# Half-array products issued in turn, an earlier load of pole planes, and two banks at the end of layer 1

## The chip, the core and the metric

The kernel runs on one core of a Trainium2 chip. The metric is the device time of one execution in microseconds (us). Engines are named PE (TensorE: matrix products; PEld are its weight loads), DVE (VectorE), ACT (ScalarE), POOL (GpSimd) and SP (SyncE, which here only issues transfers). L313 is line 313 of the kernel before.

## The reference

The input x is 16 images x 16 channels x 256 x 256, in 32-bit floats. Two layers each add a function of the group-normed x (8 groups of two channels) to x. Cut to what matters here:

```python
# layer 0, v = _gn(x)
alpha = fft2(v)
A = 1 / (omega1[:, None, None, None] - weights_pole1[None])
Bm = 1 / (omega2[:, None, None, None] - weights_pole2[None])
S = einsum('ikpq,oikp,xikq->oxik', weights_residue, A, Bm)
output_residue1 = einsum('biox,oxik->bkox', alpha, S)
C = einsum('biox,oikp->bikpx', alpha, A)
D = einsum('bikpx,xikq->bikpq', C, Bm)
output_residue2 = einsum('bikpq,ikpq->bkpq', D, weights_residue)
x = x + ifft2(output_residue1).real + pole_part(output_residue2) / Nx / Ny
# layer 1, v = _gn(x)
f = mish(conv2d(v, W1, b1))             # 3x3, each channel alone, 4 features
top, bot = upper and lower half of f
ti = involution of top with a kernel made from bot
out = mish(conv2d(concat(ti, roll(bot, -1)), W2, b2))
gate = sigmoid(3 taps over the channels of out.mean(axis=(2, 3)))
x = x + v * gate
```

The Fourier transforms are done as products with tables of cosines and sines; the spectrum is kept for 33 groups of four row frequencies.

## The kernel before

Four functions run one after the other; each takes its on-chip memory afresh, so that its first loads wait until those who last used that memory are done.

**layer0_forward** goes through 64 steps (16 images, four channels at a time). In a step, `rows` transforms the rows of the four channels (products pu and pv, lines 207 and 214) and ACT makes v from pv; `poles` multiplies v with a table into pd (line 241); and `columns` transforms the columns of the image before, two or three calls a step, into px (line 313), which ACT copies to o (line 320) and GpSimd stores to al in DRAM (line 329). The order of TensorE's instructions is written out by hand (`manual_schedule`); the other engines' orders are laid by a scheduler. The outputs pd and px have two halves of 64 partitions: a product with 64 weight columns fills the left or the right half of the array, and its output lies in partitions 0 to 63 or 64 to 127. Before, all products of one half are issued, and then all of the other: in `poles` the loop over a (the half) lies outside that over n (four products that add up), in `columns` the loop over k (the half) outside h and part. From image 1 on the steps also carry pieces of `tables`, VectorE work that makes tables for the later stages.

**layer0_mix** loads ident, ix, m8, four pieces of tt, and then the spectrum alc (eight transfers, which read al) and the pole planes av, all on SP's queue, in that order. From av VectorE makes lt (line 621); TensorE multiplies tt and lt into ps (line 635, the two halves in turn); ACT and VectorE copy ps to s (lines 643 and 645); then they spread alc into alb (lines 592 and 594); and then the products of s and alb begin (line 657). The orders of PE, ACT, DVE and POOL are by hand here.

**layer0_back** makes the new x and its norm and is not touched.

**layer1** works on nine units per image; the second convolution of an image runs while the next image's units do. After the last image only its second convolution is left: eight calls of `conv2`, each with two groups of products (line 1111, 48 records in four quarters of the array) into one bank, c2ps, whose pool `ps2` has a single buffer. ACT applies mish and adds up (line 1120). SP loads the rows that a call reads (line 1097, two buffers). Then `gate` forms the gate, and for eight parts of the image o is loaded (line 1135, four buffers), scaled four channels at a time on GpSimd (line 1158) and stored (line 1167).

Of the kernel before, what the change touches and what calls it, by code (L numbers as in the profile page):

```python
# [19 lines left out]
N = 256  # L20
G = 8
P = 128
# [50 lines left out]
def layer0_forward(ctx, tc, d, al, bd, tabs):  # L73
# [160 lines left out]
    def poles(cg, vts, acc):  # L234

        pd = psd.tile([P, 2, P], F32, tag="pd", name="pd")
        for j, vt in enumerate(vts):
            for a in range(2):
                ch = 4 * cg + 2 * j + a
                for n, (xh, k) in enumerate(((0, 0), (0, 1), (1, 0), (1, 1))):  # L240
                    nc.tensor.matmul(
                        pd[64 * a : 64 * a + 64, j],
                        lhsT=vt[:, a, xh, 64 * k : 64 * k + 64],
                        rhs=bt[:, xh, ch, 1 - k : 3 - k].rearrange("p l m -> p (l m)"),
                        start=n == 0,
                        stop=n == 3,
                    )
        gs = slice(2 * cg, 2 * cg + 2)

        def times(out, part, coef):  # L250
            shape = [P, 2, part.shape[2] // M, M]
            nc.vector.tensor_tensor(
                out.rearrange("p g (k q) -> p g k q", q=M),
                part.rearrange("p g (k q) -> p g k q", q=M),
                coef[:, gs].unsqueeze(2).to_broadcast(shape),
                ALU.mult,
            )

        t = dp.tile([P, 2, P], F32, tag="t", name="t")
# [42 lines left out]
    def columns(b, g0, rsc):  # L302

        u = us[b % 2]
        n = min(4, NF - g0)
        o = op.tile([P, 2, 2, N], F32, tag="o", name="o")
        for j in range(0, n, 2):
            lanes = 64 * min(2, n - j)
            ps = psx.tile([P, 2, 2, H], F32, tag="px", name="px")
            for k in range(min(2, n - j)):  # L310
                for h in range(2):
                    for part in range(2):
                        nc.tensor.matmul(  # L313
                            ps[64 * k : 64 * k + 64, :, h],
                            lhsT=u[:, h, part, g0 + j + k].rearrange("p f c -> p (f c)"),
                            rhs=wxn[:, h, part],
                            start=part == 0,
                            stop=part == 1,
                        )
# [228 lines left out]
def layer0_mix(ctx, tc, d, al, hd, tabs):  # L548
# [3 lines left out]
    nc = tc.nc  # L552
    nb = d["x"].shape[0]
    cp = ctx.enter_context(tc.tile_pool(name="mc", bufs=1))
    ident = load(nc, cp, d["ident"], [P, P], "ident")
    ix = load(nc, cp, d["ix"], [P, 8, N], "ix")
    m8 = load(nc, cp, d["m8"], [P, 8], "m8")

    tt = cp.tile([P, 2, C, N], F32, name="tt")
    for k in range(0, C, 4):  # L560
        nc.sync.dma_start(out=tt[:, :, k : k + 4], in_=tabs[0][:, :, k : k + 4])
    avd = tabs[1]

    alb = cp.tile([P, N, 4, nb], F32, name="alb")
    m4 = load(nc, cp, d["m4"], [P, 4], "m4")

    ap = ctx.enter_context(tc.tile_pool(name="ma", bufs=2))
    lp = ctx.enter_context(tc.tile_pool(name="ml", bufs=1))  # L570
    gp = ctx.enter_context(tc.tile_pool(name="mg", bufs=1))
    hp = ctx.enter_context(tc.tile_pool(name="mh", bufs=3))
# [31 lines left out]
    def spread(spectrum, f):  # L604
        for eng, parts in zip((nc.scalar, nc.vector), spreads[f]):
            for q, j in parts:
                expand(spectrum[q], q, j, eng)

    def load_poles(g):
        av = ap.tile([P, 32, 4, 3], F32, tag="av", name="av")  # L610
        nc.sync.dma_start(out=av.rearrange("p k f l -> p (k f l)"), in_=avd[g])
        return av

    def poles(av):

# [101 lines left out]
    E = mybir.EngineType  # L717
    with tc.manual_schedule(engines={E.PE, E.Activation, E.DVE, E.Pool}):
        spectrum = [load_spectrum(0, q) for q in range(4)]
        lt = poles(load_poles(0))  # L720
        av = load_poles(1)
        s = gp.tile([P, N, 2, C], F32, tag="s", name="s")
        for k0 in range(0, C, 2):
# [149 lines left out]
def layer1(ctx, tc, d, zn, cf, mr, nb):  # L873
# [225 lines left out]
    def conv2(b, s, acc):  # L1099
# [3 lines left out]

        begin = ((H + 1, 1, H + 2), (0, H + 1, 1))
        for q in range(2):
            ps = ps2.tile([P, 4, H], F32, tag="c2", name="c2ps")
            for blk in range(2):
                for dx in range(3):
                    x = begin[q][dx]
# [13 lines left out]
    def gate(b, acc):  # L1123
# [29 lines left out]
        for k in range(0, 8, 2):  # L1153
            following = [part(k + 2), part(k + 3)] if k < 6 else None
            c = k // 2 * 4
            for half, o in enumerate(parts):
                for i in range(4):
                    nc.gpsimd.tensor_scalar(
                        o[:, i],
                        o[:, i],  # L1160
                        scale[:, c + i : c + i + 1],
# [274 lines left out]
```

## Time and profile before

The time is 7599.57 us, the median of three runs (7587.35 to 7604.02). The profile is of an execution of 7581.6 us.

| stretch of the profile (us) | what runs |
|---|---|
| 0 to 1415 | layer0_forward |
| 1415 to 1480 | mix's loads, first tables s and alb |
| 1480 to about 2970 | layer0_mix, 33 groups |
| about 2970 to 3820 | layer0_back |
| about 3820 to 7443 | layer1, units and second convolution |
| 7443 to 7549 | second convolution of the last image, gate |
| 7549 to 7581.6 | output pass of the last image |

| line, engine | what | count | mean ns of one |
|---|---|---|---|
| L313 PE | px, 64 weight columns, 256 moving | 4224 | 385 |
| L241 PE | pd, 64 weight columns, 128 moving | 2048 | 279 |
| L635 PE | ps, 64 weight columns, 256 moving | 4224 | 384 |
| L1111 PE | c2ps, 32 weight columns, 512 moving | 12288 | 599 |
| L1120 ACT | mish of c2ps | 256 | 687 |

The mean of one is its latency: products are pipelined and those on different parts of the array overlap, so what a product costs is read from how far apart the starts lie. A view by lines gives the busy time of such a group and what ended the idle time before it; a view by stretches shows which engine is full in a stage; the timeline shows instructions in order of time, neighbours of one kind merged.

### The profile page before, as it was taken

The numbers are of one execution on the slowest core, as the hardware profiler recorded it, in microseconds if no ns is written. First come the engines' busy times: TensorE is split into PE (matmuls) and PEld (weight loads), VectorE is DVE, ScalarE is ACT, GpSimd is POOL, SyncE is SP. The second block draws the span as 40 slices with busy tenths as digits, with TensorE's granted clock in tenths as the row PEclk, the third lists the DMA queues.
The fourth block names the chain that finished last, engine by engine and source line by source line (L and its number), as shares of the span: only waits on it lengthen the run. The fifth ranks groups of instructions, "written<-read, shape, count | busy, mean of one in ns | idle before, by whom it ended". The sixth has DMA issues, their size and how long they took to land.

```text
span 7581.6 us, 148237 instructions
## 1 busy us (share of the span) xinstructions
PE 7060.1 (93%) x58664; PEld 4076.6 (54%) x58664; DVE 4908.4 (65%) x9169; ACT 3712.2 (49%) x5659; POOL 3029.4 (40%) x4126
## 2 busy tenths in 40 slices
PE   7889999799999998999979999999999999999997
PEld 5778888566667666777733333333333333333332
DVE  8999875366666665666656666666666666666662
ACT  2223333366666664111146666666666665666662
POOL 2334444211111111111135555656555666555664
PEclk9999999899999999999989999999999999999999
DMA  3444444333333335767657788888888888888886
GB/s 97 113 115 119 119 118 111 108 97 100 100 95 96 97 97 162 251 243 250 241 151 215 228 255 254 251 265 264 244 252 256 248 267 256 249 254 254 247 266 212
DMA packets 702807, 1443.62 MB, mean 190 GB/s; under 512 B 93866, under 2 KB 520038, under 8 KB 652166
## 3 DMA queue, kind: packets, MB, share of 16 engines
q1 hardware_dynamic: 557990, 959.89, 42.3%
q0 software_dynamic: 144128, 474.25, 20.4%
q8 instruction: 468, 7.67, 0.4%
q14 instruction: 221, 1.81, 0.1%
HBM read 877.25 MB, written 556.47 MB: 189 GB/s over the span
## 4 chain that ended last, share of the span: by engine, by line
PE 67%; DVE 4%; issue 3%; ACT 3%; DMA 3%; POOL 1%; SPq 0%; DVEq 0%; POOLq 0%; ACTq 0%
PE c2ps L1111 16%; PE c L969 12%; PE pd L1037 12%; PE py L837 6%; PE ph L692 5%; PE ps L635 5%; PE pg L657 4%; PE py L840 3%; ACT wide L1017 3%; DVE alb L594 2%; PE pr L996 2%; PE pf L828 1%; DMA rows<-cf 1%; PE pt L673 1%; DMA z<-zn 1%
## 5 line engine op out<-in xcount | busy, mean ns | idle before, releaser
L1017 ACT ACTIVATE wide<-c,b 32x512 f32<-32x512 f32 x2176 | 1477.4, 679 | 353.9 <-PE c L969 302.7
L1045 DVE TENSOR_TENSOR t<-pd,r 64x512 f32<-64x512 f32 x1088 | 744.2, 684 | 1286.0 <-PE pd L1037 1263.2
L1048 DVE TENSOR_TENSOR top<-pd,t 32x512 f32<-32x512 f32 x2176 | 1503.1, 691 | 52.6
L1111 PE MATMUL c2ps<-rows,c 128*32 128x512 f32 x12288 | 1391.3, 599 | 17.8 <-ACT e L1120 15.6
L969 PE MATMUL c<-z,w 102*128 102x512 f32 x2048 | 1014.7, 628 | 135.9 <-ACT wide L1017 113.8
L1029 POOL COPY wide<-wide 32x1031 f32<-32x1031 f32 (+1 forms) x576 | 568.9, 988 | 1233.5 <-ACT wide L1017 1206.2
L1037 PE MATMUL pd<-wide,dw 128*128 128x512 f32 x2048 | 1014.4, 617 | 6.5 <-DVE top L1048 2.8
L1111 PEld LDWEIGHTS c2ps<-rows,c 128*32 128x32 f32 x12288 | 392.8, 109 | 982.3 <-issue 873.9
L969 PEld LDWEIGHTS c<-z,w 102*128 102x128 f32 x2048 | 401.1, 198 | 674.3 <-issue 485.3
L1037 PEld LDWEIGHTS pd<-wide,dw 128*128 128x128 f32 x2048 | 377.1, 194 | 614.6 <-issue 446.7
L709 POOL DMA_DIRECT2D hd<-h x254 | 188.6, 743 | 1269.3 <-DVE h L705 1249.4
L1030 POOL COPY wide<-wide 32x1031 f32<-32x1031 f32 (+1 forms) x576 | 572.2, 993 | 35.6
L1120 ACT ACTIVATE e<-c2ps,b 128x512 f32<-128x512 f32 x256 | 175.9, 687 | 834.6 <-PE c2ps L1111 831.9
L313 PE MATMUL px<-wxn,u 128*64 128x256 f32 x4224 | 558.9, 385 | 2.1 <-ACT o L320 1.8
L837 PE MATMUL py<-h,iy 128*128 128x256 f32 x2048 | 541.8, 383 | 5.2 <-DMA h<-hd 5.2
L635 PE MATMUL ps<-tt,lt 128*64 128x256 f32 x4224 | 496.5, 384 | 38.9 <-DVE lt L621 34.5
L692 PE MATMUL ph<-ix,yt 64*128 64x256 f32 x4128 | 501.6, 390 | 7.1 <-issue 6.4
L313 PEld LDWEIGHTS px<-wxn,u 128*64 128x64 f32 x4224 | 401.1, 136 | 127.5 <-ACT o L320 5.4
L837 PEld LDWEIGHTS py<-h,iy 128*128 128x128 f32 x2048 | 385.2, 191 | 108.4 <-issue 44.0
L692 PEld LDWEIGHTS ph<-ix,yt 64*128 64x128 f32 x4128 | 392.2, 189 | 93.3 <-issue 46.1
L207 PE MATMUL pu<-fy,eo 128*128 128x128 f32 x2048 | 426.0, 291 | 13.0 <-DVE u L224 8.9
L988 ACT ACTIVATE bot<-c,b 128x512 f32<-128x512 f32 x544 | 343.9, 683 | 175.2 <-PE c L969 167.3
(199 smaller groups left out, 10307.1 us busy)
## 6 DMA issues: line engine op xcount, KB each, us to landing
rows<-cf SPq DMA_DIRECT2D x128, 2176.0 KB
z<-zn SPq DMA_DIRECT2D x768, 257.8 KB
cf<-top POOLq DMA_DIRECT2D x512, 240.0 KB, 7.0
cf<-bot POOLq DMA_DIRECT2D x96, 840.0 KB, 11.5
alc<-al SPq DMA_DIRECT2D x264, 256.0 KB
zn<-zb SPq DMA_DIRECT2D x128, 516.0 KB
o<-zn SPq DMA_DIRECT2D x128, 516.0 KB
z<-in_x SPq DMA_DIRECT2D x64, 1024.0 KB
```

The source lines that it names most:

```text
L313: nc.tensor.matmul(ps[64 * k : 64 * k + 64, :, h], lhsT=u[:, h, part, g0 + j + k].rearrange("p f c -> p (f c)"), rhs=wxn[:, h, part], star ...
L635: nc.tensor.matmul(ps[64 * h : 64 * h + 64, v], lhsT=lt[:, h, k, 1 - v : 3 - v].rearrange("p l f c -> p (l f c)"), rhs=tt[:, h, k], start= ...
L692: nc.tensor.matmul(ph[q][:, e], lhsT=yt[lanes, i].rearrange("p t k -> p (t k)"), rhs=ix[lanes, i], start=n == 0, stop=n == 3,)
L837: nc.tensor.matmul(py[:, yh], lhsT=iy[:, v, ys], rhs=h[:, k, v], start=v == 0, stop=False)
L969: nc.tensor.matmul(ps[:, a], lhsT=w, rhs=z[:k, c : c + 2, 0:N], start=True, stop=True)
L1017: nc.scalar.activation(self.feat[64 - 32 * q : 96 - 32 * q, f, self.groups[g], :H], ps[q][32 * f : 32 * f + 32], AF.Mish, bias=b1[0][32 * ...
L1029: nc.gpsimd.tensor_copy(flat[0:32, f, 1:m], flat[64:96, f, 0 : m - 1])
L1030: nc.gpsimd.tensor_copy(flat[96:128, f, 0 : m - 1], flat[32:64, f, 1:m])
L1037: nc.tensor.matmul(ps, lhsT=dwt if self.tail else dw, rhs=self.feat[:, f, cs, :H], start=True, stop=True,)
L1045: nc.vector.tensor_tensor(t[64:128], ps[:64], self.r[:, cs], ALU.mult)
L1048: nc.vector.tensor_tensor(self.top[32 * f : 32 * f + 32, cs, q], ps[lanes], t[lanes], ALU.add)
L1111: nc.tensor.matmul(ps[32 * j : 32 * j + 32], lhsT=c2[:, blk, dx, :], rhs=t[:, 4 * j + blk : 4 * j + blk + 4, x : x + H], start=(blk, dx) = ...
```

## The change

Four edits. In `poles` and `columns` the loop over the half becomes the innermost, so that the products go left, right, left, right; each half keeps its own order. In mix, m8 and the first av are loaded ahead of tt, and ident and ix behind it. In the last image's `conv2` the second group of each call takes a buffer of `psd` (three buffers, otherwise used for pd) in place of the single one of `ps2`. And in the last image's output pass three of the four channels of a part are scaled by VectorE, one by GpSimd. Everything that is computed stays the same.

```diff
@@ poles
-            for a in range(2):
-                ch = 4 * cg + 2 * j + a
-                for n, (xh, k) in enumerate(((0, 0), (0, 1), (1, 0), (1, 1))):
+            for n, (xh, k) in enumerate(((0, 0), (0, 1), (1, 0), (1, 1))):
+                for a in range(2):
+                    ch = 4 * cg + 2 * j + a
                     nc.tensor.matmul(
                         pd[64 * a : 64 * a + 64, j],
@@ columns
-            for k in range(min(2, n - j)):
-                for h in range(2):
-                    for part in range(2):
+            for h in range(2):
+                for part in range(2):
+                    for k in range(min(2, n - j)):
                         nc.tensor.matmul(
                             ps[64 * k : 64 * k + 64, :, h],
@@ layer0_mix
-    ident = load(nc, cp, d["ident"], [P, P], "ident")
-    ix = load(nc, cp, d["ix"], [P, 8, N], "ix")
     m8 = load(nc, cp, d["m8"], [P, 8], "m8")
+    ap = ctx.enter_context(tc.tile_pool(name="ma", bufs=2))
+    avd = tabs[1]
...
+    av = load_poles(0)
     tt = cp.tile([P, 2, C, N], F32, name="tt")
     for k in range(0, C, 4):
         nc.sync.dma_start(out=tt[:, :, k : k + 4], in_=tabs[0][:, :, k : k + 4])
-    avd = tabs[1]
+    ident = load(nc, cp, d["ident"], [P, P], "ident")
+    ix = load(nc, cp, d["ix"], [P, 8, N], "ix")
...
-        lt = poles(load_poles(0))
+        lt = poles(av)
@@ conv2
-            ps = ps2.tile([P, 4, H], F32, tag="c2", name="c2ps")
+            pool, tag = (psd, "d") if q and b == nb - 1 else (ps2, "c2")
+            ps = pool.tile([P, 4, H], F32, tag=tag, name="c2ps")
@@ gate
-                    nc.gpsimd.tensor_scalar(
+                    eng = nc.vector if i and b == nb - 1 else nc.gpsimd
+                    eng.tensor_scalar(
```

More of the change, by code (lines that the diff above doesn't have):

```diff
@@ L554, in layer0_mix, with load_poles @@
     cp = ctx.enter_context(tc.tile_pool(name="mc", bufs=1))
-    ident = load(nc, cp, d["ident"], [P, P], "ident")
-    ix = load(nc, cp, d["ix"], [P, 8, N], "ix")
     m8 = load(nc, cp, d["m8"], [P, 8], "m8")
+    ap = ctx.enter_context(tc.tile_pool(name="ma", bufs=2))
+    avd = tabs[1]
+    def load_poles(g):
+        av = ap.tile([P, 32, 4, 3], F32, tag="av", name="av")
+        nc.sync.dma_start(out=av.rearrange("p k f l -> p (k f l)"), in_=avd[g])
+        return av
+    av = load_poles(0)
     tt = cp.tile([P, 2, C, N], F32, name="tt")
@@ L561, in layer0_mix @@
         nc.sync.dma_start(out=tt[:, :, k : k + 4], in_=tabs[0][:, :, k : k + 4])
-    avd = tabs[1]
+    ident = load(nc, cp, d["ident"], [P, P], "ident")
+    ix = load(nc, cp, d["ix"], [P, 8, N], "ix")
     alb = cp.tile([P, N, 4, nb], F32, name="alb")
     m4 = load(nc, cp, d["m4"], [P, 4], "m4")
-    ap = ctx.enter_context(tc.tile_pool(name="ma", bufs=2))
     lp = ctx.enter_context(tc.tile_pool(name="ml", bufs=1))
@@ L607, in spread @@
                 expand(spectrum[q], q, j, eng)
[L609 to L612, printed above, removed]
     def poles(av):
```

## The prediction, made before the result was known

> **What bounds the kernel now.** I began with the chain of work that ended last, to see which engine sets the end:
>
> ```profile
> PE 67%; DVE 4%; issue 3%; ACT 3%; DMA 3%; POOL 1%; SPq 0%; DVEq 0%; POOLq 0%; ACTq 0%
> ```
>
> TensorE carries two thirds of it, but the four edits sit in different stages. So next the busy time of each engine in the stretches they touch (columns: stretch, its length, then PE, PEld, DVE, ACT, POOL busy with counts, TensorE clock, DMA share, GB/s):
>
> ```profile
> 552.58:1020.87 468.29, 456.45 (x4065) 392.08 (x4064) 423.88 (x1085) 178.33 (x311) 220.99 (x300) 1.00 0.44 119
> 1020.87:1370.34 349.47, 349.47 (x3194) 304.34 (x3193) 187.30 (x568) 107.31 (x213) 166.15 (x234) 1.00 0.40 107
> 147.92:552.58 404.66, 356.58 (x2825) 311.72 (x2824) 371.62 (x1104) 110.35 (x205) 146.05 (x200) 0.92 0.41 114
> 1415.50:1480.30 64.80, 17.43 (x133) 10.32 (x136) 23.70 (x25) 19.67 (x15) 4.39 (x8) 0.65 0.44 156
> 7442.80:7548.70 105.90, 87.34 (x771) 24.52 (x770) 4.79 (x14) 15.23 (x35) 31.96 (x56) 1.00 0.64 211
> 7548.70:7581.60 32.90, 0.00 (x0) 0.00 (x0) 0.00 (x0) 0.00 (x0) 23.82 (x40) 0.50 0.57 192
> ```
>
> In the forward stage, 1020.87 to 1370.34 is pure TensorE (349.47 of 349.47; 19 steps of four channels), 147.92 to 552.58 is VectorE's (92%, 16 steps), and 552.58 to 1020.87 lies between (PE 97%, DVE 91%, 24 steps). The start of mix has TensorE working 17 of 65 us. In the tail it works 87 of 106; in the output pass GpSimd works alone.
>
> One forward step's half-array part, on TensorE's timeline (start, length, line, tiles, count):
>
> ```profile
> 1057.02 2.24 PE L241 MATMUL pd<-bt,v 128*64 128x128 f32 x29
> 1058.99 0.43 PE L313 MATMUL px<-wxn,u 128*64 128x256 f32 x1
> 1059.10 0.38 PE L241 MATMUL pd<-bt,v 128*64 128x128 f32 x2
> ...
> 1059.47 7.90 PE L313 MATMUL px<-wxn,u 128*64 128x256 f32 x62
> 1067.30 0.38 PE L34 MATMUL gn_mean<-mv,ones 128*128 128x2 f32 x2
> ```
>
> A written product is two records (two passes). The 32 pd and 64 px passes take 1057.02 to 1067.30, 10.28 us. The halves do overlap already: the first px pass, on the left half, starts before pd's last ones on the right. Read one by one, the starts go in fours: px starts come in twins, 6 ns apart, at 1003.42, 1004.34 and 1005.26, each half making four passes 0.216 apart with one interval of 0.267 where the halves change over, so eight passes take 0.920, where pairs of 0.216 would take 0.862. And since one half runs four passes behind the other, the burst's first four and last four run alone.
>
> Mix's residues already alternate the halves:
>
> ```profile
> 1821.85 1.95 PE L635 MATMUL ps<-tt,lt 128*64 128x256 f32 x16
> 1823.72 3.73 PE L692 MATMUL ph<-ix,yt 64*128 64x256 f32 x32
> ```
>
> Sixteen passes of px's shape from 1821.85 to 1823.72, 1.87 us with the turnaround; record by record pairs start every 0.216 with no interval missed but the first, 0.267.
>
> **What the Trainium skill says.** "TensorE: Matmul & The Clock Gate", Part 3, says that weight loads overlap running matmuls only when the row group differs, and that matmuls start in strict order. Here it does not hold: px at 1058.99 precedes pd at 1059.10, and ps pairs with different *column* halves run at 0.216. "TensorEngine Tiling (Array Packing)", Key Properties, says that tiles load weights and multiply independently; that agrees. "DMA: Bandwidth & Descriptors", Queues, rings and completion order, says each DMA engine consumes descriptors in ring order; it agrees with av, issued at 1436.81 behind 7 MB and used at 1447.38. "SBUF — State Buffer", two separate sides, says VectorE in a two-port mode and GpSimd exclude each other on a shared port pair; no run here shows it yet.
>
> **Forward products.** Alternating: pd 16 pairs x 0.109 (its passes' interval) = 1.74; px 32 pairs x 0.216 = 6.91; turnaround after the last pair, 0.09 over an interval (1067.30 less the last px start, 1066.99, is 0.31); two first intervals, 0.05 each; and a wait for v of the second half, ready at 0.89 (ACT 1057.21 for 0.69) plus a semaphore, when the first eight pairs are through at 0.92: 0.05. Sum 8.9, against 10.28: 1.4 us a step. No instruction is added on any engine.
> - 19 pure TensorE steps and the last: 20 x 1.4 = 28. VectorE has 187 of 349 there, so nothing takes over.
> - 24 mixed steps: 24 x 1.4 = 34 if all counted, but 468 - 34 = 434 would ask VectorE for 424 of 434. In the VectorE-bound stretch it reached 92%; at 92 to 95% the floor is 446 to 461. Gain 7 to 22; I take 14.
> - 16 VectorE-bound steps: TensorE waits there already; 0 to 6, taken 2.
> - the last image's columns after 1385: pairs save 2, but o's two buffers wait for their stores (ACT waited 7.8 on al<-o at 1422.97): 1.
>
> Forward 45, between 28 and 60.
>
> **Mix's start.** VectorE's first work and the sync queue before:
>
> ```profile
> 1447.38 3.70 DVE L621 TENSOR_TENSOR lt<-av,m 128x512 f32<-128x512 f32 x6 [64.92 <-DMA av<-avd]
> 1468.31 11.74 DVE L594 TENSOR_SCALAR alb<-alc,m 128x1024 f32<-128x1024 f32 x10
> 1479.86 2.48 DVE L621 TENSOR_TENSOR lt<-av,m 128x512 f32<-128x512 f32 x4
> ...
> 1429.79 6.94 SPq L582 DMA_DIRECT2D alc<-al  x8
> 1436.81 14.62 SPq L611 DMA_DIRECT2D av<-avd  x3
> ```
>
> Now: av lands 1447.4, residues and their copies to 1468.3, the spread to 1480.05, first mix product 1480.25. After: m8 and av (0.2 MB) are issued first at 1415.6 and land by about 1419; lt is done by 1423; the first piece of tt lands by 1422. But the first copy into s waits, in the program as built, for the semaphores of the last al stores (its memory overlaps what these read), which arrived at 1429.7; alc's issue waits for the same. So four k (psg's buffers) are computed early, and the other twelve follow from 1429.8: two to three at half clock, 1.7 each, the rest 0.86: 13 us, to 1443. The spread's quarters of alc stream in order behind the same bytes as before, so the last still lands by 1447, ahead of its use; 11.7 us more give 1454.6. Gain 25. If s did not wait, the bound is the landing of alc: 28; if every late k runs at half clock: 20. Moving ident and ix behind tt costs nothing: they are first needed at 1495, and 420 GB/s bring them by 1435.
>
> **Tail of layer 1.** The 16 product groups of the last image and the store loop:
>
> ```profile
> 7508.07 5.41 PE L1111 MATMUL c2ps<-rows,c 128*32 128x512 f32 x48 [0.96 <-ACT e L1120]
> 7514.43 5.42 PE L1111 MATMUL c2ps<-rows,c 128*32 128x512 f32 x48 [0.95 <-ACT e L1120]
> ...
> 7548.70 2.19 POOL L1158 TENSOR_SCALAR o<-o,scale,mean 128x258 f32<-128x258 f32 x4 [59.48 <-DVE scale L1151]
> 7551.19 0.79 POOL L1167 DMA_DIRECT2D out_dram<-o  x1 [0.30 <-POOL o L1158]
> 7552.02 2.19 POOL L1158 TENSOR_SCALAR o<-o,scale,mean 128x258 f32<-128x258 f32 x4
> ```
>
> Each group waits for the activation of the one before, the bank being single: 6.38 apart. With a second bank, 12 rounds of four quarters, whose starts lie 0.431 apart, are 5.2: 1.2 x 16 = 19 at most. The loads of rows then set the pace: a load (2176 KB) takes 8.4 alone but about 11 while the image before is being stored (7458 to 7500, DMA 96% busy), and one issue at 7456.7 stands behind o loads on the in-order sync queue. Followed step by step, rows of s=2 land at 7467.5 (start then, 7469.72 now: 2 gained), s=5 lands about 7503.7 (now 7508.07: 4 gained), and only the last three steps run free, 2.1 each: 10.5. Between 8 and 17.
>
> Output pass: a part now costs GpSimd 2.19 + 0.30 + 0.79 = 3.3 us. After, one row group on GpSimd (0.55), three on VectorE (about 0.35 each, from L515's 128x256), the wait and the issue: 1.7 to 2.3. Then the four reloads decide, each behind the store that frees its buffer (3.4 from issue to landing), 3.5 to 4 to arrive: last store issued at +17, landed at +21 to 22, for 32 now. Bytes agree: 6.3 MB at 400 GB/s are 16. Gain 10; 7 if the port pair serialises VectorE and GpSimd, 13 if the 2.7 us before the last store goes too. The new bank and the VectorE rows add waits, but behind them nothing else is queued.
>
> Sum: 45 + 25 + 10.5 + 10 = 91: 7600 - 91 = 7509, say 7508.
>
> **Rivals.**
> - *VectorE takes what TensorE gives.* For it: 91% busy over the mixed steps. Against: 19 steps at 54%. With only a fifth of the forward's gain: 9 + 45.5, 7545.
> - *Everything counts*, the mixed steps in full and rows never late: 28 + 34 + 6 + 28 + 17 + 13 = 126, 7474. Against: the VectorE sums above.
> - *Slower.* If two halves' weights cannot load together, each 64-column load (0.137) would follow the other: pairs of 0.274, 48 x 0.274 = 13.2 a step, 2.9 more, over 44 steps 128; less 45.5: 7682. Against: ps does it at 0.216.
>
> **How the numbers follow.** Forecast 0.75, first rival 0.14, second 0.06, slower 0.03; 0.02 for gains so far eaten that nothing is measured. The time is the forecast's. Adding the ends of the forward term (17 either way) and those of the others in quadrature gives some 20 about 7508; up to 7542 it takes in half of the first rival, down to 7484 the nearer part of the second.
>
> **What will show it.** px starting every 0.216 in pairs; the pure steps 16.7 us instead of 18.07, the mixed ones bound by VectorE at about 95%; first pg product 25 us closer to the last px; groups of c2ps 5.2 apart except where rows<-cf is named; last store 21 us after scale. The forecast fails if the pure steps keep their length (the halves were not the limit), or if ACT's drain of px becomes the wait.

## The result and the profile after

The changed kernel takes 7524.26 us, the median of five runs (7514.01 to 7531.52); the kernel before took 7599.57. The ratio is 0.9903, with a 95% interval of 0.9886 to 0.992: about 75 us less (61 to 87), where 91 were forecast. The direction and the places are as forecast, and the time lies in the range, but three of the four terms came out smaller.

The profiled execution of the changed kernel lasts 7527.5 us. Line numbers move a little: px stays L313; lt is L623 and ps L637; in layer 1 c2ps is L1115, e L1124, rows L1099, the loads of o L1139, the scaling L1163, the store L1172. First the stretches that answer to those of the prediction (stretch, length, then PE, PEld, DVE, ACT, POOL busy with counts, TensorE clock, DMA share, GB/s):

```profile
148.20:552.50 404.30, 339.18 (x2825) 285.26 (x2824) 371.03 (x1104) 110.18 (x205) 145.70 (x200) 0.91 0.41 114
552.50:1015.50 463.00, 429.64 (x4066) 354.01 (x4064) 418.65 (x1085) 177.44 (x310) 220.71 (x300) 0.98 0.45 121
1015.50:1341.40 325.90, 325.90 (x3194) 270.59 (x3192) 187.32 (x568) 107.30 (x213) 166.13 (x234) 1.00 0.43 114
1382.90:1422.10 39.20, 17.05 (x131) 11.28 (x128) 23.63 (x25) 19.68 (x15) 4.40 (x8) 0.74 0.73 248
7398.50:7498.30 99.80, 88.38 (x771) 31.67 (x770) 4.88 (x14) 15.23 (x35) 31.96 (x56) 0.94 0.67 224
7498.30:7527.50 29.20, 0.00 (x0) 0.00 (x0) 9.46 (x25) 0.00 (x0) 11.47 (x16) 0.50 0.62 216
```

A step is counted here from its first pd product to that of the next. Line by line against before: the VectorE-bound steps keep their length (404.3 for 404.7), the mixed ones lose 5 us (463.0 for 468.3), the pure ones 24 (325.9 for 349.5). The start of mix, from the last px to the first product of mix, is 39 for 65, the tail of layer 1 is 100 for 106, the output pass 29 for 33. In the mixed steps TensorE's busy time fell by 27 us (456.5 to 429.6), but the steps shortened by 5: TensorE now waits for 33 us where it waited for 12. That is where the largest missing piece of the gain went. (The tail's line also has a lower TensorE clock, 0.94 for 1.00; this comes back below.)

Half-array part of one pure step, TensorE's timeline after (start, length, line, tiles, count):

```profile
1048.92 2.04 PE L241 MATMUL pd<-bt,v 128*64 128x128 f32 x32
1050.79 7.08 PE L313 MATMUL px<-wxn,u 128*64 128x256 f32 x64
1057.79 0.38 PE L34 MATMUL gn_mean<-mv,ones 128*128 128x2 f32 x2
```

From 1048.92 to 1057.79 are 8.87 us; before it took 10.28, and 8.9 were forecast.

The last image's second convolution and the output pass after, on TensorE's and GpSimd's timelines (in brackets the idle time before, and what ended it):

```profile
7398.60 21.12 PE L1115 MATMUL c2ps<-rows,c 128*32 128x512 f32 x192
7424.76 33.71 PE L1115 MATMUL c2ps<-rows,c 128*32 128x512 f32 x288 [5.03 <-DMA rows<-cf]
7462.13 33.05 PE L1115 MATMUL c2ps<-rows,c 128*32 128x512 f32 x288 [3.66 <-DMA rows<-cf]
```

```profile
7498.48 0.55 POOL L1163 TENSOR_SCALAR o<-o,scale,mean 128x258 f32<-128x258 f32 x1 [53.78 <-DVE scale L1155]
7500.56 0.79 POOL L1172 DMA_DIRECT2D out_dram<-o  x1 [1.53 <-issue]
...
7508.39 0.67 POOL L1163 TENSOR_SCALAR o<-o,scale,mean 128x258 f32<-128x258 f32 x1 [1.77 <-DMA o<-zn]
...
7522.77 0.80 POOL L1172 DMA_DIRECT2D out_dram<-o  x1 [3.42 <-issue]
```

Groups of 48 products now run back to back in blocks of 4, 6 and 6; the wait for ACT's e (0.95 before each group) is gone and two waits for rows stand in its place. In the output pass the fifth part waits for its reload, and the last store for 3.42 us of "issue", which is no wait that the profile can name.

One thing in this trace misleads. Layer 1's body, from the first to the last start of the products c<-z,w of its first convolution, which no edit touches, is 3573.6 us here and 3560.5 in the trace of before: the spans of the two profiled executions differ by 54 us only, not 75. The experiments show that this follows no edit.

### The profile page after: what moved, and what is told of

It reads as the page before. It is cut to its first block, busy times and chain, and to the rows that moved or that the text cites. A ratio compares the mean times of both kernels' runs of the same rounds, so it can differ in the third digit from the quotient of the medians.

```text
span 7527.5 us, 148267 instructions
## 1 busy us (share of the span) xinstructions
PE 6993.6 (93%) x58664; PEld 3984.4 (53%) x58664; DVE 4913.0 (65%) x9193; ACT 3712.1 (49%) x5659; POOL 3016.3 (40%) x4102
## 4 chain that ended last, share of the span: by engine, by line
PE 76%; DVE 12%; DMA 4%; ACT 3%; issue 3%; SPq 0%; POOL 0%; DVEq 0%; ACTq 0%; POOLq 0%
PE c2ps L1115 17%; PE c L971 12%; PE pd L1039 12%; PE py L839 6%; PE ph L694 5%; PE ps L637 5%; PE pg L659 4%; PE py L842 3%; PE px L313 3%; ACT wide L1019 3%; PE pu L207 2%; DVE alb L601 2%; PE pv L214 2%; PE pr L998 2%; DMA rows<-cf 1%
## 5 line engine op out<-in xcount | busy, mean ns | idle before, releaser
L1115 PE MATMUL c2ps<-rows,c 128*32 128x512 f32 x12288 | 1395.2, 601 | 20.6 <-DMA rows<-cf 20.6
L1115 PEld LDWEIGHTS c2ps<-rows,c 128*32 128x32 f32 x12288 | 402.4, 109 | 978.7 <-issue 902.4
L1124 ACT ACTIVATE e<-c2ps,b 128x512 f32<-128x512 f32 x256 | 175.9, 687 | 840.0 <-PE c2ps L1115 837.3
L637 PE MATMUL ps<-tt,lt 128*64 128x256 f32 x4224 | 495.2, 384 | 12.8 <-DMA tt<-td 9.3
L313 PE MATMUL px<-wxn,u 128*64 128x256 f32 x4224 | 482.2, 379 | 10.0 <-ACT o L320 10.0
L207 PE MATMUL pu<-fy,eo 128*128 128x128 f32 x2048 | 432.4, 295 | 26.3 <-DVE u L224 21.6
L694 PEld LDWEIGHTS ph<-ix,yt 64*128 64x128 f32 x4128 | 390.5, 189 | 90.4 <-issue 43.9
L214 PE MATMUL pv<-at,eo 128*128 128x128 f32 x2048 | 419.5, 289 | 0.0
## 6 DMA issues: line engine op xcount, KB each, us to landing
cf<-bot POOLq DMA_DIRECT2D x96, 840.0 KB, 11.6
```

What stands on the lines that cost most here:

```text
L207: nc.tensor.matmul(pu[:, xh, e].rearrange("p v m -> p (v m)"), lhsT=lhs, rhs=fy[:, e], start=True, stop=True,)
L313: nc.tensor.matmul(ps[64 * k : 64 * k + 64, :, h], lhsT=u[:, h, part, g0 + j + k].rearrange("p f c -> p (f c)"), rhs=wxn[:, h, part], star ...
L637: nc.tensor.matmul(ps[64 * h : 64 * h + 64, v], lhsT=lt[:, h, k, 1 - v : 3 - v].rearrange("p l f c -> p (l f c)"), rhs=tt[:, h, k], start= ...
L694: nc.tensor.matmul(ph[q][:, e], lhsT=yt[lanes, i].rearrange("p t k -> p (t k)"), rhs=ix[lanes, i], start=n == 0, stop=n == 3,)
L1115: nc.tensor.matmul(ps[32 * j : 32 * j + 32], lhsT=c2[:, blk, dx, :], rhs=t[:, 4 * j + blk : 4 * j + blk + 4, x : x + H], start=(blk, dx) = ...
```

## The experiments

Stretches of every profiled execution are set side by side at the end of this section.

**Each edit alone, on the kernel before.** Forward only, then mix only, the bank only, the output split only; each is the hunk of the diff above with that name:

```diff
@@ forward alone: columns, and poles likewise
-            for k in range(min(2, n - j)):
-                for h in range(2):
-                    for part in range(2):
+            for h in range(2):
+                for part in range(2):
+                    for k in range(min(2, n - j)):
@@ mix alone: and ident, ix behind tt
+    av = load_poles(0)
...
-        lt = poles(load_poles(0))
+        lt = poles(av)
@@ bank alone
-            ps = ps2.tile([P, 4, H], F32, tag="c2", name="c2ps")
+            pool, tag = (psd, "d") if q and b == nb - 1 else (ps2, "c2")
+            ps = pool.tile([P, 4, H], F32, tag=tag, name="c2ps")
@@ split alone
-                    nc.gpsimd.tensor_scalar(
+                    eng = nc.vector if i and b == nb - 1 else nc.gpsimd
+                    eng.tensor_scalar(
```

> The kernel before with only the forward stage's products issued in turn (poles and columns). Theory (TensorE pays for halves that change in blocks, and what VectorE-bound steps gain is lost): 28 to 36 us faster, the pure steps 16.7 us with 64 px passes and about 19.1 with 72, the mixed steps 5 to 6 us shorter in all. Rival (the whole of the forecast's 45 was there and something else in the changed kernel ate it): 42 to 48 us faster. Layer 1 and mix keep their lengths; if the length of layer 1's units moves by ten us in this trace too, that is a spread between executions and no effect of an edit.

> The kernel before with only the order of mix's first loads changed. Theory: the wait for the pole planes falls away and the copies into s wait for the last al stores: last px to first pg product falls from 65 to about 39, 24 to 28 us faster. Rival (part of that is owed to the shorter forward end, whose last stores come earlier): under 20 us faster here.

> The kernel before with only the second bank for the last image's c2ps. Theory (the loads of rows take the place of the bank wait): groups 5.2 apart but for three gaps of 2 to 5 us on the rows loads, first group to the scale 4 to 8 us shorter, total 4 to 8 us faster. Rival (the bank was the only limit): 16 to 19 us faster, groups 5.2 apart throughout.

> The kernel before with only the last image's output pass split between VectorE and GpSimd. Theory (the chain store, landing, reload, scale sets the pace): scale to end 29 us in place of 33, 3 to 5 us faster. Rival (GpSimd was the limit and the rest of the changed kernel hid it): 9 to 13 us faster, scale to end 20 to 24.

Measured, as ratios to the kernel before: forward 0.9959 (0.9947 to 0.9971), about 31 us; mix 0.9964 (0.9952 to 0.9977), 27; bank 0.9988 (0.9982 to 0.9995), 9; split 0.9994 (0.9986 to 1.0001), 5, which by itself can't be told from nothing. The sum, 72, agrees with the 75 of the whole, though each of these figures has an interval of 5 to 10 us either way, so that a loss of ten us between edits would not show in the times. The stretches say it more closely: with one edit alone, the stretch that it touches is within 3 us of the changed kernel's, so none eats much of another's gain. Forward's rival (45 are there and hidden) falls. So does mix's: with the old forward stage, last px to first pg is still 39.1. The length that mix's theory gave holds, but not the wait that it named: the last al store had landed 0.7 us before the first copy into s, which began 0.2 us after the first product group ps was done (more on this below). For bank and split the theories hold. The bank's trace shows the same sort of waits as the changed kernel's:

```profile
7449.47 21.11 PE L1113 MATMUL c2ps<-rows,c 128*32 128x512 f32 x192
7475.82 22.45 PE L1113 MATMUL c2ps<-rows,c 128*32 128x512 f32 x192 [5.25 <-DMA rows<-cf]
7500.36 10.67 PE L1113 MATMUL c2ps<-rows,c 128*32 128x512 f32 x96 [2.09 <-DMA rows<-cf]
7512.81 31.51 PE L1113 MATMUL c2ps<-rows,c 128*32 128x512 f32 x288 [1.77 <-DMA rows<-cf]
```

**The left-over group of columns.** The ninth call of `columns` has one group of four, so eight passes on the left half and none on the right. Steps with it (72 px passes) went from 19.7 to only 19.1 us, while the others went from 18.07 to 16.66.

```diff
@@ columns
+            if n - j == 1:
+                for part in range(2):
+                    for h in range(2):
+                        nc.tensor.matmul(
+                            ps[64 * h : 64 * h + 64, :, h],
+                            lhsT=u[:, h, part, g0 + j].rearrange("p f c -> p (f c)"),
...
+                for h in range(2):
+                    nc.scalar.activation(
+                        o[:64, j // 2, :, H * h : H * h + H],
+                        ps[64 * h : 64 * h + 64, :, h],
...
```

> The changed kernel, with the one group that is left over in the ninth call of columns put on both halves of the array: its products for h = 0 left, for h = 1 right, so that its eight passes make four pairs, and ACT copies it in two instructions of half the size. Theory (steps with 72 px passes gained only 0.6 us because these eight passes run alone, 8 x 0.216, where before they overlapped the backlog of the other half): these steps fall from 19.1 to about 18.25 us, five of them in the pure part, one at the end and a share of the ten others: 4 to 9 us faster than the changed kernel. Rival (such a step is held by ACT, which copies three tiles more): no change, or 1 to 3 us slower by the added copy.

Measured 7517.14, ratio 0.9901 (0.9884 to 0.9917), where the changed kernel has 0.9903: the times can't tell a gain. The trace can. Steps with 72 px passes are 18.24 us in the pure part, as expected, and ACT's second copy delays nothing. Last px comes 7.7 us earlier, but only some 3 us of that are the edit's: steps 44 to 61 last 307.4 for 309.7 us and the end of the stage 1.0 less. The rest lies before step 20, where the traces scatter by as much; the mixed steps gain nothing (463.7 for 463.0). So the 4 to 9 us of the theory are not shown, its account of the step is. The timelines of such a step's end, changed kernel and then this one, show where:

```profile
1073.71 2.54 PE L313 MATMUL px<-wxn,u 128*64 128x256 f32 x14
1076.18 0.38 PE L34 MATMUL gn_mean<-mv,ones 128*128 128x2 f32 x2
```

```profile
1070.67 0.60 PE L331 MATMUL px<-wxn,u 128*64 128x256 f32 x4
1071.10 1.03 PE L313 MATMUL px<-wxn,u 128*64 128x256 f32 x8
1072.07 0.38 PE L34 MATMUL gn_mean<-mv,ones 128*128 128x2 f32 x2
```

The eight passes of the left-over group (L313 in the second) take about 0.97 us in pairs, counted to the start of the next product (1071.10 to 1072.07); alone they took 8 x 0.216 = 1.73.

**Eight o buffers.**

```diff
-    op = ctx.enter_context(tc.tile_pool(name="l1o", bufs=4))
+    op = ctx.enter_context(tc.tile_pool(name="l1o", bufs=8))
```

> The changed kernel with eight o buffers in layer 1 in place of four, so that no load of o waits for a store of the same image. Theory (the reload behind each store sets the output pass, and o loads that wait on SP's queue hold the loads of rows behind them in the tail): scale to end from 29 to 19 to 22 us, the gap on rows at the seventh pair of groups gone, 8 to 14 us faster than the changed kernel. Rival (bytes bind, the DMA being full in both stretches): output pass shorter but the tail longer by the loads that move into it, within 4 us of the changed kernel.

Measured 7509.18, ratio 0.9889 (0.9874 to 0.9904): 11 us under the changed kernel by the ratios, 15 by the medians; the two intervals overlap. What the trace shows of it is the output pass, which falls from 29.2 to 21.7 us; the tail is as long as in the changed kernel (100.1 for 99.8), with TensorE still waiting for rows, 10.1 us in three gaps. So the theory is right on the output pass and wrong on the tail, where the rival is right: the DMA engines are full from 7406 to 7446 (346 GB/s), as they were in the changed kernel from 7418 to 7458, and o loads that need not wait any more take their bytes earlier (six are issued from 7428.20 on). In the output pass GpSimd's own loop and the two "issue" gaps remain:

```profile
7497.38 0.56 POOL L1163 TENSOR_SCALAR o<-o,scale,mean 128x258 f32<-128x258 f32 x1
7498.23 0.79 POOL L1172 DMA_DIRECT2D out_dram<-o  x1 [0.30 <-POOL o L1163]
...
7504.02 0.79 POOL L1172 DMA_DIRECT2D out_dram<-o  x1 [2.69 <-issue]
```

**Less table work on VectorE, before and after.** Both kernels have this cut out of `tables`:

```diff
-            nc.vector.tensor_scalar(n, arg, 1.0 / TWO_PI, phase, ALU.mult, ALU.add)
...
-            nc.scalar.activation(n, arg, AF.Sin)
...
-            exponential(nc, tp, af)
...
-            nc.vector.tensor_tensor(arg, arg, n, ALU.mult)
```

> The kernel before, with the VectorE and ACT work of the exponential tables left out (from the scaling of the argument to the last product; a first product is stored in their place, so the output is not the reference's). It is the base of the next run. About 10.7 us of VectorE work less for each of 16 pieces. Steps 20 to 43 should then last about 18.07 us each (TensorE alone), 433 in place of 468; the total 30 to 45 us under before.

> The changed kernel with the same work left out (output not the reference's). Theory (in the mixed steps VectorE and what waits on it took what TensorE gave): with VectorE relieved, steps 20 to 43 are now 26 to 32 us shorter than in the run above, where the full kernels differ by 5, and the two runs' totals differ by 95 to 105 us, where the full kernels differ by 75. Rival (something else in these steps, such as the drain of px, holds them): the difference over these steps stays at 5 to 10 us and the totals differ by 75 to 80.

Measured 7560.37 (7551.97 to 7563.41) and 7461.7 (7459.67 to 7469.54): 98.7 us apart, inside the theory's 95 to 105 and outside the rival's 75 to 80. Steps 20 to 43, before and after:

```profile
550.50:995.80 445.30, 445.30 (x4066) 388.03 (x4065) 243.96 (x750) 136.92 (x272) 214.85 (x300) 1.00 0.44 120
```

```profile
536.50:952.70 416.20, 416.20 (x4065) 345.69 (x4064) 243.74 (x750) 136.74 (x272) 214.78 (x300) 1.00 0.47 128
```

TensorE is busy all the time in both, and 29.1 us of the products' saving are kept, where the full kernels differ by 5.3. (The base was put too low, at 433: it leaves out one step in four with 72 passes, and the pt products.) Steps 4 to 19 gain 12 us here, for nothing in the full kernels. ACT's work for the same tables is cut too, so what is shown is that the tables' work holds these steps, VectorE and its Sin on ACT together.

**The output pass of image 14 left out**, to see what makes the rows late:

```diff
-        parts = [part(0), part(1)]
+        parts = [part(0), part(1)] if b != nb - 2 else None
...
+        if b == nb - 2:
+            return
         for k in range(0, 8, 2):
```

> The changed kernel with the output pass of the last image but one left out (eight loads of o and eight stores, which run beside the last image's second convolution; that image is not written, so the output is not the reference's). Theory (the loads of rows lose time to this traffic and stand behind its o loads on SP's queue; that is what the tail waits for once the bank is doubled): the three gaps on rows in the last image's 16 groups shrink to under 2 us in all, groups 5.2 apart throughout, first group to scale 87 to 90 us in place of 100, 8 to 13 us faster than the changed kernel. Rival (the rows loads are late by their own chain, issue and landing, whatever else is under way): gaps of 5 us and more stay, under 4 us faster.

Measured 7513.77, ratio 0.9884 (0.9869 to 0.9899). All 16 groups in one block:

```profile
7396.08 83.62 PE L1115 MATMUL c2ps<-rows,c 128*32 128x512 f32 x768
```

No gap is left; first group to scale is 86.9, for 99.8. The rows are late because of that image's output pass, and the rival falls. That is 14 us under the changed kernel by the ratios and 10 by the medians. Of the 12.9 us of the tail, 8.7 are the two waits for rows; 3.9 more, by estimate, are half clock. About and after each of the two waits TensorE's granted clock was halved for a while (columns as above):

```profile
7422.50:7429.30 6.80, 4.54 (x24) 1.36 (x28) 0.00 (x0) 0.00 (x0) 6.12 (x11) 0.50 0.99 317
7463.40:7466.80 3.40, 3.40 (x20) 1.16 (x16) 0.00 (x0) 0.00 (x0) 0.00 (x0) 0.50 1.09 348
```

There the rounds of four quarters start 0.85 us apart, and 0.43 elsewhere; the group after the first wait takes 7.40 us and the one after the second 6.87, where the others take 5.2 (hence the 3.9). Without image 14's output the clock stays at 1.00 through all 16 groups, as it does before, where a wait of 0.95 stands ahead of each group. In the changed kernel SP's queue shows one way in which the rows come late:

```profile
7438.07 13.58 SPq L1139 DMA_DIRECT2D o<-zn  x4
7451.75 23.07 SPq L1099 DMA_DIRECT2D rows<-cf  x3
```

Four o loads hold SP's queue for 13.6 us, because they wait for buffers (the last two are issued 0.06 us after a store of image 14 has landed), and the next rows are issued only after the last. But with eight buffers they waited less and the tail was no shorter. So the queue alone does not set it; that the rest is bandwidth fits the full DMA engines, but how the two share it was not taken apart.

**Tables spread over more steps.** Two tries for a kernel that gets the lost forward gain back. Both contain the left-over group's edit; the second also has eight o buffers.

```diff
@@ first: pieces at the end of a step
-    with tc.manual_schedule(engines={mybir.EngineType.PE}):
+    with tc.manual_schedule(engines={mybir.EngineType.PE, mybir.EngineType.DVE}):
...
             if i >= 4:
-                next(pieces, None)
+                credit += 6.3
+                while credit > 0:
+                    credit -= next(pieces, 1e9)
@@ second: finer pieces in the middle of a step, by hand from step 2 on
+            if i >= 2:
+                credit += 7.1
+                while credit >= 2.5:
+                    credit -= next(pieces, 1e9)
             v1 = rows(b, cg, 1, *now)
```

> The changed kernel with the ninth call of columns on both halves, as in the run of the lone group, and VectorE's work for the tables spread evenly over steps 4 to 61 in place of 4 to 43: the generator hands out finer pieces (one k of the residue tables, one g of the poles, half a pair of the exponentials), the loop takes about 6.3 us of them per step, VectorE's order is written out by hand, and av has two buffers. All is computed. VectorE then has about 16.5 us of work in each step, TensorE 16.7 to 19. Theory (TensorE's saving is lost only where VectorE's work piles up): steps 4 to 61 last 17.5 to 19.5 us each, 1010 to 1130 in all for 1155 to 1175 now, 50 to 130 us faster than the lone-group kernel (that one 7517). Rival (a fixed order on VectorE makes each step wait for its late operands): within 20 us of the lone-group kernel, or slower.

> The kernel of the run above, with the tables' VectorE work spread over steps 2 to 62 as in the run of the spread tables, but: the pieces come in the middle of a step (after the group norm scalars of the next step, ahead of the second half of u) and no longer at its end, they are finer (3.6, 1.6, 3.4, 4.0, 4.7 and 5.5 us, some 7.1 a step), te and wt have two buffers, and VectorE's order is by hand from step 2 on only, so that the start stays as it was. Theory (in the spread run TensorE's gn_var waited 133 us behind pieces that stood ahead of gnq on VectorE; even spreading helps once no short operation that TensorE waits for stands behind a piece): steps 4 to 61 last 17.5 to 19.5 us each, last px at 1230 to 1330 in place of 1375, 7390 to 7470 in all. Rival (VectorE at 16.8 us a step against TensorE's 16.7 to 18.2 leaves no slack for any fixed order): last px at 1375 or later, no gain over the run above or slower.

Both are slower: 7693.11, ratio 1.0123 (1.0106 to 1.014), and 7852.01, ratio 1.034 (1.0324 to 1.0355); last px at 1555 and 1723 in place of 1383. So both rivals were right on the times. (In the first, 29 us of this lie before the first pd and 24 in steps 0 to 3, where the order by hand holds too. Steps 4 to 19 did become shorter, 367.0 us for 401.1 in the kernel that it was built on; those after them lost it.) What TensorE waited for most (total, times, longest; 200 to 1500 in the first try, 200 to 1600 in the second):

```profile
PE gn_var L42 <- DVE gnq L39: 154.7, 44, 10.7
```

```profile
PE gn_mean L34 <- DVE mv L176: 287.3, 45, 10.9
```

In the first, a piece stands ahead of gnq, in the second ahead of mv: short operations of the group norm for which TensorE stands still. (For gnq it also waited 58 us in the kernel that the first was built on; for mv it did not wait there.) Most steps last 20 to 31 us, with VectorE busy for 15 to 26 of them. The waits cost clock as well: over the whole execution it was 0.959 and 0.948, for 0.968 and 0.966 in the profiled kernels that these were built on, which is at most 70 and 140 us by estimate (the difference times the span). My costs were off as well: the exponential pieces, put at 4.5 and 6.2, had VectorE busy in single steps for 25 us. So the order that the scheduler lays, pieces mixed with the step's operations one by one, is better than either of mine. Whether a third order would win the gain that the less-tables pair shows stays open.

**Both helpful edits together.**

```diff
@@ columns, as above
+            if n - j == 1:
...
@@ layer1
-    op = ctx.enter_context(tc.tile_pool(name="l1o", bufs=4))
+    op = ctx.enter_context(tc.tile_pool(name="l1o", bufs=8))
```

> The changed kernel with both edits that helped: the left-over group of columns on both halves, and eight o buffers in layer 1. They touch different stages, so their gains (7 and 15 us by the medians) should add: 7498 to 7508, ratio to before 0.987 to 0.989. Rival (part of either gain was spread between executions): 7508 to 7515.

Measured 7505.75 (7497.7 to 7514.6), ratio 0.988 (0.9864 to 0.9897): in the theory's band and the lowest median here of the kernels that compute everything; against the eight buffers alone the difference (3 by the medians, 7 by the ratios) is not resolved, and the interval of the ratio still touches the changed kernel's (0.9886 to 0.992). Its last px comes 2.0 us before the changed kernel's: steps 44 to 61 keep their saving (307.4), the mixed steps, at 467.3, give nothing.

**All profiled executions.** From their traces, in us; body is layer 1 from the first to the last start of c<-z,w, tail from the last image's first c2ps to scale, out from scale to the end.

```
                         last px   px to pg   body     tail    out
before                   1415.2    65.1       3560.5   105.7   33.0
changed                  1382.9    39.2       3573.6    99.8   29.2
forward alone            1380.7    66.0       3570.3   105.8   34.8
mix alone                1412.6    39.1       3557.3   106.4   33.4
bank alone               1412.8    65.8       3566.9    98.1   33.1
split alone              1414.8    65.7       3572.1   107.4   28.8
left-over group          1375.3    40.6       3560.6   103.3   28.6
eight o buffers          1383.9    39.2       3558.5   100.1   21.7
before, less tables      1389.9    66.5       3561.6   106.1   33.4
changed, less tables     1319.8    38.8       3567.0   100.6   29.1
without image 14's out   1380.2    39.2       3570.1    86.9   30.8
both edits               1381.0    40.2       3561.3   102.2   21.7
tables spread, first     1555.3    38.6       3559.8    98.7   28.4
tables spread, second    1723.2    38.5       3561.2   100.6   21.3
```

Body lies between 3557 and 3574 in kernels whose body is the same and follows no edit; that is the 13 us by which the two first traces misled. Each kernel was profiled once, so this does not tell builds from executions; but the times of one kernel scatter as much (the changed one's from 7514.01 to 7531.52). Means over the rows with and without an edit, the two spread kernels left out, give its size better than one pair: mix 26.3, bank 5.6 (five rows without, six with, which scatter from 98 to 103; the row without image 14's output left out), split 4.2 (the two eight-buffer rows left out), forward 32 (full tables and left-over group as it was). Sum 68, within the interval of the ratio. The 75 may be a little high: the medians of the kernel before, taken again beside the experiments, lie from 7590.64 to 7600.98.

## Why the prediction was right or wrong

**Forward, 45 forecast, 32 measured.** The mechanism is right: pairs of 0.216, and 8.87 us in place of 10.28. By terms:
- *Pure steps, "20 x 1.4 = 28"*: 23.6 over 19 steps, 27 by the forecast. The figure of 1.4 was read from one step and used for all. One step in four has a left-over group on one half. In the old order these eight passes ran beside the backlog of the other half; in turn, they run alone. The prediction had even noted that "the burst's first four and last four run alone", yet priced no step with an odd group. The left-over run settles it: put on both halves, such a step falls to 18.24.
- *Mixed steps, "7 to 22; I take 14"*: 5.3, under its own low end, and the largest miss. Over all traces with full tables it is smaller still: 463.0 to 466.6 (four kernels with the products in turn, columns otherwise as they are, mean 464.7) for 466.9 to 468.3 (four without, 467.4). The step that failed is "at 92 to 95% the floor is 446 to 461". VectorE's share did not rise: 423.9 of 468.3 before is 90.5%, 418.7 of 463.0 after is 90.4%. The share of 92% came from another stretch with other neighbours and was lent to this one. Counted from a step's first row product (pu), the loss has a pattern: from step 24 to 43 every second step keeps its saving (mean 17.02 us for 18.47) and the one after it grows (21.39 for 20.57). What TensorE waits for there, before and after (total, times, longest):

```profile
PE pu L207 <- DVE u L224: 6.4, 6, 2.2
PE px L313 <- ACT o L320: 1.8, 2, 1.5
```

```profile
PE pu L207 <- DVE u L224: 19.4, 12, 2.3
PE px L313 <- ACT o L320: 9.1, 7, 2.1
```

  The first is VectorE itself. The second was the prediction's "if ACT's drain of px becomes the wait", in part: ACT works only 177 of 463 us, but stands 14.0 us before Sin, waiting for VectorE's arg (the argument of a table's sine), and each of the seven waits for o comes right behind such a Sin. That VectorE's table work and this Sin hold these steps is shown by the less-tables pair (29.1). Why VectorE stops at 90%, its own waits after the change tell: these four, with 2.7 us for gn_mean, make 40 of the 44 us in which it stands idle:

```profile
DVE arg L515 <- DMA ed<-arg: 10.9, 9, 2.7
DVE st L174 <- DMA z<-in_x: 9.3, 6, 3.0
DVE arg L525 <- ACT n L523: 9.2, 10, 1.5
DVE u L224 <- ACT right L222: 7.5, 10, 1.4
```

  The first is the tables again: arg has one buffer, and the next piece waits until the last one's store (ed) is through. In step 33 VectorE stands 2.70 us for it (until 797.36), the products' u comes after it, and TensorE's pu waits 2.29 us (until 800.51). Four of the twelve waits for u, 7.2 us of 19.4, follow such a stand; ahead of the other eight VectorE was busy throughout. A second buffer for arg was not tried alone. Clock is lost here too: four stretches of half clock, 17 us in all, stand in these steps after and none before. What they cost was not taken apart, but the left-over kernel has more of it (0.96 over these steps for 0.98) and takes no longer (463.7).
- *VectorE-bound steps, 2*: 0.4, within "0 to 6". *Last columns, 1, and the last step, 1.4*: 3.3 together.

The first rival, *VectorE takes what TensorE gives*, was right in the main for steps 4 to 43 and wrong for the pure ones.

**Mix's start, 25 forecast, 26 measured.** The first step is right: the wait for av is gone, and av was used 4 us after last px. The sum is right in part by luck, since two errors cancel. The forecast let the copies into s wait for the last al stores, 14.6 us after last px, with four k's computed ahead, and gave the rest 13 us. In the trace the last al store lands after 10.4 us (first alc issue at 1393.5). What came last was tt: its first piece was there only 9.4 us after last px, forecast 7; the first ps product started at 1392.67, its group was done at 1394.64, and the first copy began at 1394.80. So no k came early, all sixteen took 15.5 us, and the copies ended at 27.4, forecast 27.9; the spread ended at 39.0, forecast 39.5. The profile puts the wait of both down to tt:

```profile
1392.67 3.68 PE L637 MATMUL ps<-tt,lt 128*64 128x256 f32 x16 [9.33 <-DMA tt<-td]
1393.48 11.56 SPq L589 DMA_DIRECT2D alc<-al  x8
1394.80 1.01 ACT L647 COPY s<-ps 128x512 f32<-128x512 f32 x1 [7.99 <-DMA tt<-td]
```

The kernel with mix's edit alone shows the same order (store 11.6, group 12.2, copy 12.3 us after last px). Whether the copies would have waited for the stores, had tt come sooner, no run shows.

**Tail, 10.5 forecast, 5.6 measured.** The bank was doubled and the rows took its place, as said. Two terms were off (s numbers the eight calls of conv2 from 0). One is the loads: rows of s = 2 came 26.2 us after the first group (forecast 24.6) and those of s = 5 63.5 after (forecast 60.8). The load of s = 5 is the first of the three rows shown above, issued at 7451.75 behind the four o loads. The other was put at nothing: about each wait TensorE's clock was halved, so that the last six groups, forecast to run free, took 33.05 us where the bank-alone kernel's last six took 31.51. Of the 4.9 us that are missing, 2.7 lie before s = 5, and 1.7 are this last half clock. I had priced a load at 11 us beside image 14's stores; the run without that image's output shows that its traffic is all that keeps 13 us more from coming.

**Output pass, 10 forecast, 4 measured, under the range given for it.** VectorE and GpSimd do work at once: the GpSimd rows take 0.55 to 0.73 for 0.55 alone, and VectorE's 24 take 9.12 us with eight buffers, 0.38 each. So the exclusion of which the Trainium skill ("SBUF — State Buffer", two separate sides) speaks for VectorE's two-port mode is not what costs the time here: at most 0.18 us of a GpSimd row can be its. Whether VectorE was in that mode no run here shows. The failing term is the chain of store and reload: "each behind the store that frees its buffer (3.4 from issue to landing)" holds for the first two, whose reloads were issued 3.5 and 3.7 us after their stores, but the third and fourth followed by 5.5 and 7.2, with the DMA engines 97 to 98% busy (7504 to 7516). And "3.5 to 4 to arrive" became 4.3, 6.4, 6.4 and 5.6 from a reload's issue to its scaling. With 3.42 us of "issue" before the last store, where 2.7 stood in the profile of before, it is issued at +24.3 and not at +17. (The first store, at +2.1 after its 1.53 us of "issue", is within the 1.7 to 2.3 of the forecast: VectorE's three rows fall into that time.) Eight buffers remove the chain and give 7.5 more, which brings the pass near the 13 that the forecast had as its best end; the "issue" gaps stay.

**Slower, by loads of weights that serialise:** refuted by the 0.216 pairs in px, as by ps before.

Taken together: 13 us too much in forward, 5 in the tail, 6 in the output pass, 1 too little in mix: 68 for 91 by the stretches, 75 by the medians.

## What to carry to other kernels

A saving on one engine is worth what its neighbour in the same steps leaves: read that neighbour's share in the very stretch, and ask what it stands idle for. Where that is its own stores, loads and partners, as here, take its present share and not a higher one as the ceiling. Before a per-step saving is multiplied, look for steps of another shape. Where a second buffer removes a wait, look at the load that feeds the same stage: here it was the next limit, and it competed with what the image before was still writing. A long wait can cost more than its own length: here the two for rows brought 3.9 us of half clock, the fifteen short ones for the bank none. And when a forecast comes out right, check its waits one by one; mix's start was right through two errors that cancelled.

## What was not expected of the hardware

- Eight passes on one half of the array alone cost 1.73 us and about 0.97 as pairs, but behind a backlog on the other half they had been cheaper: steps with them fell by 0.6 where the others fell by 1.4.
- TensorE's granted clock was 0.50 for 6.8 and 3.4 us about and after the tail's waits of 5.03 and 3.66 us, and rounds of products took 0.85 us there for 0.43; fifteen waits of 0.95 before left it at 1.00.
- The last store of the output pass is issued late with nothing named: the gap is 2.69 us with eight buffers, about 2.7 before, 3.42 after and in the split-alone and left-over kernels, and 1.02 in the run without image 14's output. No run here explains it.
- Layer 1's body differs by up to 16 us (0.5%) between profiled executions of kernels that no edit there tells apart, more than two of the four edits are worth together.
- A fixed order on VectorE with evenly spread work cost 176 and 346 us against the kernels that it was built on: TensorE stood 155 and 287 us for short operations that came behind long ones, and its clock fell besides.
